# Convolution behind a group normalization: the first load of image 0 in two transfers

## The chip, the cores and the metric

The kernel runs on one core of a Trainium2 chip. A core has a matrix engine (TensorE, in the profile PE), a vector engine (VectorE, DVE), an activation engine (ScalarE, ACT), a general engine (GpSimd, POOL) and a sync engine (SP) that here issues all transfers. Data move between the chip's main memory and the on-chip memory (128 partitions) through sixteen DMA engines. The metric is the time of one execution in device microseconds, the median of several. For the kernel before it is 83.69 us (three executions, 83.59 to 84.02 us).

## The reference

The input `x` holds 8 images of 32 channels and 128 x 128 pixels in float32. Cut to what matters:

```python
def _gn(v, G=16, eps=1e-5):                 # mean and variance over 2 channels x 128 x 128 pixels
    g = v.reshape(B_, G, C_ // G, H_, W_)
    m = jnp.mean(g, axis=(2, 3, 4), keepdims=True)
    s = jnp.var(g, axis=(2, 3, 4), keepdims=True)
    return ((g - m) / jnp.sqrt(s + eps)).reshape(v.shape)

# a 3x3 convolution by FFT of size 256, cut to 128 x 128 at an offset of 64
sp = jnp.fft.ifft2(fout, norm='ortho').real
sh = (fft_H - out_h) // 2
sw = (fft_W - out_w) // 2
out = sp[:, :, sh:sh + out_h, sw:sw + out_w]
out = out + bias[None, :, None, None]

x = x + conv(_gn(x), L0_conv_weight, L0_conv_bias)
```

The offset of the cut makes the convolution reach only a quarter of the output; the rest of an image gets the bias alone. Every pixel is read once and written once: 16.8 MB in, 16.8 MB out.

## The kernel before

On the host, `x` is brought into the shape (4 pairs, 128 partitions, 2 images, 64 rows, 64 columns). A partition holds one channel at one parity of row and column. So one image is 128 partitions x 4096 numbers, and half an image 128 partitions x 2048 numbers (8192 bytes a partition).

All loads are issued by the sync engine one after the other, each with a semaphore of its own. Images 0 and 1 come in halves of 32 rows, the weights behind the first half:

```python
def load(to, of):
    name = f"load{len(put.sems)}"
    put.semaphore(name)
    return put("sp", lambda sp: sp.dma_start(to, of), adds=name)

for img in range(2):
    loaded[img] = []
    for half in range(2):
        rows = slice(half * H // 2, (half + 1) * H // 2)
        loaded[img].append((rows.stop, load(xts[img][:, rows, :], x[0, :, img, rows, :])))
        if img == 0 and half == 0:
            weights_in = load(wb_sb, wb)
for img in range(2):
    loaded[2 + img] = [(H, load(xts[2 + img], x[1, :, img]))]
for pair in range(2, NPAIR):
    loaded[2 * pair] = loaded[2 * pair + 1] = [(H, load(pairs[pair], x[pair]))]

def rows_in(img, last):          # the loads that hold rows before `last`
    return [token for k, (_, token) in enumerate(loaded[img]) if k == 0 or loaded[img][k - 1][0] < last]
```

The first instructions that need data wait for what `rows_in` names. For image 0 these are a small product on TensorE that estimates the mean (`pilot`), the sum of each half on VectorE and, with the origin from the pilot, the sum of squares of each half on ScalarE:

```python
def pilot(img):
    pilot_ok[img] = put(
        "pe", lambda e: e.matmul(ps_w[:, img : img + 1], avg, xts[img][:, 0, 0:1], start=True, stop=True),
        *rows_in(img, 1), avg_ok, mark=True,
    )
...
# sum_up(img), for each half k of image 0
e.tensor_reduce(to_sum(img, k)[:, 0:1], piece, mybir.AxisListType.X, ALU.add)      # waits rows_in(img, rows.stop)
# sum_squares(img)
e.activation(unused[...], piece, AF.Square, bias=origins[img], accum_out=to_sum(img, k)[:, 1:2])
```

From the sums follow mean and deviation (`group`, `take_std`), the normalized quarter `g` of the image (`normalize`), then twelve products per image on TensorE into PSUM (`multiply`, three chunks of four taps) and the addition to `x` (`add`). GpSimd adds the bias to the rest. The main loop works on one image while it prepares the next. Finished images go out through the same sync engine:

```python
def store(to, of, *needs):
    return put("sp", lambda sp: sp.dma_start(to, of), *needs, adds="stored")
...
xt, to = xts[B - 1], out[NPAIR - 1, :, 1]
store(to[:, N:H, :], xt[:, N:H, :], biased[B - 1][0])
add(B - 1, 0, 2)
add(B - 1, 2, NCHUNK)
stored = store(to[:, 0:N, :], xt[:, 0:N, :], biased[B - 1][1], *added[B - 1])
```

The kernel ends when all stores have landed.

Of the kernel before, what the change touches and what calls it, by code (L numbers as in the profile page):

```python
# [33 lines left out]
P = 128  # L34
# [113 lines left out]
def conv_preact_kernel(nc: bass.Bass, x: bass.AP, wb: bass.AP, out: bass.AP):  # L148
    NPAIR, _, _, H, W = x.shape
# [7 lines left out]
    def sbuf(name, *shape):  # L157
        return nc.alloc_sbuf_tensor(name, list(shape), F32).ap()
# [6 lines left out]
    pairs = [sbuf(f"x{pair}", P, 2, H, W) for pair in range(NPAIR)]  # L165
    xts = [pairs[img // 2][:, img % 2] for img in range(B)]
# [3 lines left out]
    loaded = {}  # L170
# [7 lines that stand above are left out]
        loaded[img] = []  # L178
        for half in range(2):
            rows = slice(half * H // 2, (half + 1) * H // 2)  # L180
            loaded[img].append((rows.stop, load(xts[img][:, rows, :], x[0, :, img, rows, :])))
            if img == 0 and half == 0:
                weights_in = load(wb_sb, wb)
    for img in range(2):
        loaded[2 + img] = [(H, load(xts[2 + img], x[1, :, img]))]
    for pair in range(2, NPAIR):
        loaded[2 * pair] = loaded[2 * pair + 1] = [(H, load(pairs[pair], x[pair]))]

    def rows_in(img, last):

        return [token for k, (_, token) in enumerate(loaded[img]) if k == 0 or loaded[img][k - 1][0] < last]

# [1 line left out]
    pair = sbuf("pair", P, P // 2, 2)  # L196
    w_sb = sbuf("w_sb", P, 4 * P)
    eps = sbuf("eps", P, 1)
    half = sbuf("half", P, 2 * C)
# [47 lines left out]
    def take_first(img, *needs):  # L247

        first_ok[img] = put(
            "pool", lambda e: e.tensor_copy(sums[(img - 1) % 2][:, 2:3], xts[img][:, 0, 0:1]),  # L250
            *rows_in(img, 1), *needs, *([group_ok[img - 3]] if img > 3 else []), mark=True,
# [8 lines that stand above are left out]
# [15 lines left out]
    def sum_up(img):  # L275
        sums_ok.setdefault(img, [])
        for k, rows in enumerate(parts(img)):
            piece = xts[img][:, rows, :].rearrange("p h w -> p (h w)")
            sums_ok[img].append(
                put(  # L280
                    "dve",
                    lambda e: e.tensor_reduce(to_sum(img, k)[:, 0:1], piece, mybir.AxisListType.X, ALU.add),  # L282
                    *rows_in(img, rows.stop), *([group_ok[img - 2]] if img > 1 else []), mark=True,
                )
            )
# [276 lines left out]
```

## Time and profile before

The page describes one execution, its span is 82.2 us.

| | kernel before |
|---|---|
| median time | 83.69 us |
| span of the profiled execution | 82.2 us |
| TensorE, VectorE, ScalarE, GpSimd busy | 81%, 61%, 58%, 37% of the span |
| DMA engines busy | 97.0% of the time of all sixteen |
| moved | 33.62 MB, mean 409 GB/s |
| first load (1024 KB): issued, landed | 0.81 us, 5.79 us |
| last store (1056 KB): issued, from issue to landing | 75.66 us, 6.5 us |

In the chain of waits each line has a start, a length and what ran, in microseconds from the start of the span. In the answers by window each line has the window, its length, the busy time (and number of instructions) of PE, PE's weight loads, DVE, ACT and POOL, then the granted clock of TensorE as a share, the busy share of the DMA engines and the GB/s that they moved. In short windows the share can exceed 1, since packets of one engine overlap a little. In the row of tenths one digit stands for a fortieth of the span.

### The profile page before, as it was taken

What the parts mean: (1) busy time and instruction counts of PE and PEld (TensorE: products, weight loads), DVE (VectorE), ACT (ScalarE), POOL (GpSimd) and SP (SyncE); (2) the same over time, 40 slices, a digit from 0 to 9 for tenths busy, and PEclk for the clock granted to TensorE, in tenths of its full rate; (3) what the DMA queues carried; (4) which work ended last, traced back from release to release, by engine and by line L of the source; (5) the groups of instructions that cost most, each with busy time, mean ns of one, the idle gap of its engine ahead of it and who ended that gap; (6) DMA issues with size and microseconds to landing.
All of it is one profiled execution on the core that took longest, in us unless ns stands there. A gap on an engine that the chain in (4) does not pass through costs nothing.

```text
span 82.2 us, 684 instructions
## 1 busy us (share of the span) xinstructions
PE 66.5 (81%) x222; PEld 41.3 (50%) x222; DVE 50.2 (61%) x43; ACT 48.0 (58%) x55; POOL 30.3 (37%) x41
## 2 busy tenths in 40 slices
PE   0019974999999999999999999999999999990000
PEld 0014443566666666666666666666666666650000
DVE  0019845971999499689949967994998341007000
ACT  6108957982797499479939956993896530000000
POOL 6808500000069910108984910770193059000000
PEclk9999998589999999999999999999999999999965
DMA  2899999999979979989959889999979999999994
GB/s 40 319 406 414 422 426 442 454 414 422 526 335 510 478 319 478 494 367 414 510 255 510 383 383 510 414 399 462 494 311 414 454 414 430 454 406 434 398 433 201
DMA packets 2208, 33.62 MB, mean 409 GB/s; under 512 B 256, under 2 KB 288, under 8 KB 416
## 3 DMA queue, kind: packets, MB, share of 16 engines
q1 hardware_dynamic: 2208, 33.62, 97.0%
HBM read 16.84 MB, written 16.78 MB: 409 GB/s over the span
## 4 chain that ended last, share of the span: by engine, by line
PE 75%; ACT 7%; DMA 6%; DVE 3%; issue 1%
PE ps L399 73%; DMA x<-x_dram 6%; ACT unused L302 5%; DVE x L415 2%; PE ps_m L317 2%; ACT g L360 1%; PE ps_w L257 1%; ACT std L340 0%; ACT square L329 0%; DVE rstd L346 0%; DVE var L334 0%; ACT origin L291 0%; DVE rstd L343 0%
## 5 line engine op out<-in xcount | busy, mean ns | idle before, releaser
L399 PE MATMUL ps<-g,w_sb 128*128 128x363 f32 (+1 forms) x192 | 60.7, 473 | 1.1 <-ACT g L360 1.1
L399 PEld LDWEIGHTS ps<-g,w_sb 128*128 128x128 f32 x192 | 36.0, 193 | 21.1 <-ACT origin L291 1.6
L282 DVE TENSOR_REDUCE sums<-x 128x1 f32<-128x4096 f32 x7 | 30.9, 4411 | 0.8 <-DMA x<-x_dram 0.8
L302 ACT ACTIVATE unused<-x,origin 128x4096 f32<-128x4096 f32 (+1 forms) x9 | 30.0, 3330 | 0.3
L381 POOL TENSOR_SCALAR x<-x,bias_sb 128x1984 f32<-128x1984 f32 (+3 forms) x12 | 23.2, 1949 | 18.1 <-ACT origin L291 13.8
L415 DVE SCALAR_TENSOR_TENSOR x<-ps,bias_sb,x 128x1089 f32<-128x1089 f32 (+2 forms) x9 | 10.9, 1221 | 7.6 <-PE ps L399 7.6
L360 ACT ACTIVATE g<-x,rstd 128x1089 f32<-128x1089 f32 (+2 forms) x9 | 10.7, 1201 | 3.9 <-DVE rstd L346 3.9
L282 DVE TENSOR_REDUCE first_sums<-x 128x1 f32<-128x2048 f32 x2 | 4.6, 2286 | 6.2 <-DMA x<-x_dram 6.2
L250 POOL COPY sums<-x 128x1 f32<-128x1 f32 x6 | 1.0, 185 | 18.0 <-DMA x<-x_dram 18.0
L334 DVE TENSOR_SCALAR var<-ps_m,square 128x1 f32<-128x1 f32 x8 | 1.7, 218 | 7.6 <-ACT square L329 7.6
L329 ACT ACTIVATE square<-ps_m,origin 128x1 f32<-128x1 f32 x8 | 2.1, 261 | 7.0 <-PE ps_m L317 7.0
L257 PE MATMUL ps_w<-x,avg 128*128 128x1 f32 x4 | 0.8, 278 | 5.9 <-DMA x<-x_dram 5.9
L433 PE MATMUL ps<-x,avg 128*128 128x512 f32 x6 | 4.9, 942 | 0.0
L257 PEld LDWEIGHTS ps_w<-x,avg 128*128 128x128 f32 x4 | 0.9, 250 | 6.4 <-issue 6.4
L317 PEld LDWEIGHTS ps_m<-sums,avg 128*128 128x128 f32 x16 | 2.8, 189 | 2.2 <-DVE x L415 1.0
L340 ACT ACTIVATE std<-var,eps 128x1 f32<-128x1 f32 x8 | 2.4, 294 | 2.3 <-DVE var L334 2.3
L343 DVE RECIPROCAL rstd<-std 128x1 f32<-128x1 f32 x8 | 1.3, 164 | 2.9 <-ACT std L340 2.9
L291 ACT ACTIVATE origin<-ps_w 128x1 f32<-128x1 f32 x2 | 0.3, 158 | 4.2 <-PE ps_w L257 4.2
L462 POOL COPY w_sb<-wb_sb 32x128 f32<-32x128 f32 (+1 forms) x8 | 2.5, 341 | 0.0
L317 PE MATMUL ps_m<-sums,avg 128*128 128x3 f32 x16 | 2.3, 214 | 0.0
L433 PEld LDWEIGHTS ps<-x,avg 128*128 128x128 f32 x6 | 1.5, 287 | 1.0 <-issue 1.0
L346 DVE TENSOR_SCALAR rstd<-ps_m,rstd 128x1 f32<-128x1 f32 x8 | 1.8, 219 | 0.3
(19 smaller groups left out, 10.4 us busy)
## 6 DMA issues: line engine op xcount, KB each, us to landing
x<-x_dram SPq DMA_DIRECT2D x2, 4096.0 KB, 33.6
out_dram<-x SPq DMA_DIRECT2D x2, 4096.0 KB, 16.4
out_dram<-x SPq DMA_DIRECT2D x3, 2048.0 KB, 9.1
x<-x_dram SPq DMA_DIRECT2D x4, 1024.0 KB, 7.8
x<-x_dram SPq DMA_DIRECT2D x2, 2048.0 KB, 17.4
out_dram<-x SPq DMA_DIRECT2D x1, 1056.0 KB, 6.5
out_dram<-x SPq DMA_DIRECT2D x1, 992.0 KB, 11.0
wb_sb<-wb_dram SPq DMA_DIRECT2D x1, 62.0 KB, 5.0
```

The lines of the kernel that those rows point to most:

```text
L257: "pe", lambda e: e.matmul(ps_w[:, img : img + 1], avg, xts[img][:, 0, 0:1], start=True, stop=True),
L282: lambda e: e.tensor_reduce(to_sum(img, k)[:, 0:1], piece, mybir.AxisListType.X, ALU.add),
L302: lambda e: e.activation(unused[:, rows.start * W : rows.stop * W], piece, AF.Square, bias=origins[img], accum_out=to_sum(img, k)[:, 1:2],),
L317: lambda e: e.matmul(ps_ms[:, 0 : of.shape[1]], avg, of, start=(part == 0), stop=(part == last)),
L329: lambda e: e.activation(squares[img], ps_ms[:, 0:1], AF.Square, bias=origins[img]),
L340: lambda e: e.activation(stds[img], variances[img], AF.Sqrt, bias=eps, scale=float(FFT * FFT)),
L360: lambda e: e.activation(g[:, rows, :], xt[:, LO + rows.start : LO + rows.stop, LO:W], AF.Identity, bias=rstd[:, 1:2], scale=rstd[:, 0:1],),
L381: put("pool", lambda e: e.tensor_scalar(part, part, 1.0, bias_sb, op0=ALU.mult, op1=ALU.add), *free, mark=mark)
L399: lambda e, k=k, dc=dc, rows=rows, top=top: e.matmul(ps[:, 0:rows, 0 : N - dc], w_sb[:, k * P : (k + 1) * P], g[:, top : top + rows, dc:N] ...
L415: lambda e: e.scalar_tensor_tensor(part, in0=ps, scalar=bias_sb, in1=part, op0=ALU.add, op1=ALU.add),
L433: "pe", lambda e: e.matmul(pss[1][:, 0, :], avg, piece, start=True, stop=True),
L462: lambda e: e.tensor_copy(w5[to, :, dc, :, c.start * C : c.stop * C], taps[:, 1 - rin : 5 - rin, b, :].rearrange("p (dr r) b o -> p dr r ( ...
```

## The change

The first half of image 0 is no longer one transfer of 128 partitions. It becomes a transfer of partitions 0 to 15, which gives each of the sixteen DMA engines a single row of 8192 bytes, and behind it a transfer of the other 112 partitions. The aim is that the engines get their first packets sooner. All other loads stay as they are. `loaded` now remembers the first row of each piece instead of the row behind its last, so that `rows_in` can name both pieces of the first half; for the other loads it names the same ones as before.

```diff
         for half in range(2):
             rows = slice(half * H // 2, (half + 1) * H // 2)
-            loaded[img].append((rows.stop, load(xts[img][:, rows, :], x[0, :, img, rows, :])))
+
+            for part in (slice(0, 16), slice(16, P)) if img == half == 0 else (slice(0, P),):
+                token = load(xts[img][part, rows, :], x[0, part, img, rows, :])
+                loaded[img].append((rows.start, token))
             if img == 0 and half == 0:
                 weights_in = load(wb_sb, wb)
     for img in range(2):
-        loaded[2 + img] = [(H, load(xts[2 + img], x[1, :, img]))]
+        loaded[2 + img] = [(0, load(xts[2 + img], x[1, :, img]))]
     for pair in range(2, NPAIR):
-        loaded[2 * pair] = loaded[2 * pair + 1] = [(H, load(pairs[pair], x[pair]))]
+        loaded[2 * pair] = loaded[2 * pair + 1] = [(0, load(pairs[pair], x[pair]))]
 
     def rows_in(img, last):
 
-        return [token for k, (_, token) in enumerate(loaded[img]) if k == 0 or loaded[img][k - 1][0] < last]
+        return [token for first, token in loaded[img] if first < last]
```

## The prediction

> **What bounds the kernel now.** I read three things in this order: what the DMA engines do over the whole span, the chain of waits together with its end, and the first microseconds in windows. First, from the page:
>
> ```profile
> span 82.2 us, 684 instructions
> PE 66.5 (81%) x222; PEld 41.3 (50%) x222; DVE 50.2 (61%) x43; ACT 48.0 (58%) x55; POOL 30.3 (37%) x41
> ...
> DMA  2899999999979979989959889999979999999994
> ...
> q1 hardware_dynamic: 2208, 33.62, 97.0%
> ```
>
> The packets of the only DMA queue fill 97.0% of the time of sixteen engines; TensorE is busy for 81%. The row of tenths has a low first slice, a slightly low second one, and then nothing that looks like a long pause until the last slice. The chain of work that ended last tells another story at first sight:
>
> ```profile
> 0.81 4.99 DMA x<-x_dram
> ...
> 13.43 6.17 PE ps L399 x14
> ...
> 71.11 3.01 PE ps L399 x10
> ...
> 74.15 1.48 DVE x L415 x2
> ```
>
> It says: wait for the first half of image 0 until 5.79 us, then statistics, then TensorE without a pause, then the last addition until 75.63 us. The span ends at 82.2 us, 6.5 us later, and the chain names no compute for that rest. The last store and the windows around it show why:
>
> ```profile
> 75.66 0.33 SPq L423 DMA_DIRECT2D out_dram<-x  x1
> ```
>
> ```profile
> 43.00:74.10 31.10, 31.10 (x111) 19.43 (x109) 20.05 (x18) 18.60 (x21) 12.46 (x10) 1.00 0.99 427
> 74.10:76.00 1.90, 0.01 (x1) 0.00 (x0) 1.48 (x2) 0.00 (x0) 0.00 (x0) 1.00 1.03 440
> 76.00:79.00 3.00, 0.00 (x0) 0.00 (x0) 0.00 (x0) 0.00 (x0) 0.00 (x0) 0.92 0.97 409
> 79.00:81.20 2.20, 0.00 (x0) 0.00 (x0) 0.00 (x0) 0.00 (x0) 0.00 (x0) 0.50 0.96 407
> ```
>
> The last column is GB/s, the one before it the busy share of the DMA engines. The last store (1056 KB) is issued at 75.66 us, but from 76 to 79 us the engines are still full with earlier stores. 1056 KB at the 427 GB/s of the steady stretch take about 2.5 us, so its data start near 81.2 - 2.5 = 78.7 us, although by the first load's example (issue 0.81, first packet about 1.82 us) it could have started near 76.7 us. So there are about 2 us of slack between the compute chain and the end. **The bound is the DMA stream**: it starts at 1.82 us, moves 33.62 MB, and never runs dry. What moves the end is the point at which each engine reaches its full rate, not the time at which the first tile lands. A shift of the first landing by less than 2 us changes the end only so far as it shifts the stream too.
>
> Now the start, in windows:
>
> ```profile
> 0.00:1.80 1.80, 0.00 (x0) 0.00 (x0) 0.00 (x0) 1.00 (x1) 1.13 (x7) 1.00 0.00 0
> 1.80:2.20 0.40, 0.00 (x0) 0.00 (x0) 0.00 (x0) 0.39 (x2) 0.33 (x2) 1.00 1.51 266
> 2.20:2.60 0.40, 0.00 (x0) 0.00 (x0) 0.00 (x0) 0.10 (x1) 0.40 (x1) 1.00 0.62 123
> 2.60:3.00 0.40, 0.00 (x0) 0.00 (x0) 0.00 (x0) 0.00 (x0) 0.32 (x2) 1.00 0.71 287
> 3.00:3.40 0.40, 0.00 (x0) 0.00 (x0) 0.00 (x0) 0.00 (x0) 0.32 (x2) 1.00 0.99 410
> 3.40:5.20 1.80, 0.00 (x0) 0.00 (x0) 0.00 (x0) 0.00 (x0) 0.60 (x2) 1.00 1.00 416
> ```
>
> Nothing moves before 1.8 us, the stream has its steady 410 GB/s only from 3.0 us. A packet is counted where it starts (nine packets of 8192 bytes start before 2.0 us, which is the 369 GB/s that the window 1.8 to 2.0 shows). In the trace's packet records the sixteen engines start their first packets between 1.82 and 2.35 us, on average 0.20 us after the first; these first packets take 0.37 to 1.17 us, 0.76 us on average, where a packet of the same size later takes 0.309 us. So the ramp costs an engine 0.20 us of stagger and 0.76 - 0.31 = 0.45 us of a slow first packet, about **0.65 us** in all. That is the whole pot of this change: 0.8% of the run. A gain over 2% (1.7 us) isn't there to be had.
>
> [...]
>
> **The change part by part.**
> Bytes: none added; 33.62 MB as before. Packets: the same 128 rows of 8192 bytes, and one more completion per engine at 9 ns: 0.01 us.
> Issue: one more DMA on the queue of the sync engine. The first was issued at 0.81 us, the second at 1.25 us, so one issue costs 0.44 us there. The 112 rows are issued at about 1.25 us, the weights and the rest 0.44 us later than before (last issue about 5.2 + 0.4 us instead of 5.2). The engines then hold work for tens of microseconds (the last load lands at 43 us), so only the 112 rows feel it: with the 1.01 us from issue to first packet they can start at about 2.26 us, and the last engine about 0.5 us later, 2.75 us.
> First packet: [...] I expect the stagger to shrink from 0.20 us to about 0.05 us on average: -0.15 us.
> Sharing: [...] For the engine that is last, nearly nothing, 0.0 to 0.1 us.
> The other 112: [...] One such meeting costs up to one packet, 0.31 us; I count half to one and a half of them for the engine that is last: 0.15 to 0.45 us. From the weights on the order is the old one, and each engine carries its delay to the end.
> Sum for the last engine, if the ports rule: +0.05 + 0.3 + 0.01, about **+0.4 us**.
> Waits: TensorE's first pilot product and VectorE's first sum wait for two semaphores instead of one; the list of instructions is otherwise the same on each engine, apart from the new wait. A few tens of ns, on the side with 2 us of slack: 0. First landing 5.79 us becomes about 6.1 us, and the TensorE chain shifts from 13.43 to about 13.8 us, also inside the slack.
>
> **The rivals.**
> *Rival 1, [...].* If the first packets are slow [...], then one row each starts all engines early, and the 112 rows arrive behind them in time. For it: the stagger of 0.5 us, and the very first packet, which took only 0.37 us. Against it: the durations don't grow in the order of the starts (the second packet to start took 0.91 us, the thirteenth 0.74 us). Then the stagger falls (-0.15 us) and up to half of the slow first packet (-0.2 us): 0.2 to 0.4 us below 83.69 us, 83.3 to 83.5 us.
> *Rival 2, hidden anyway.* The slow first reads belong to the first touch of the memory by each engine and stay, and the 112 rows come at 2.26 to 2.75 us, no sooner than the engines would have been free. The stagger moves from the first packet to the second: within 0.1 us of 83.69 us.
> *Rival 3, the queue's hole.* If the second transfer is served later than 2.75 us (a ramp of its own), each engine idles after its one packet; 0.2 to 0.6 us worse, and with the shared ports up to 84.5 us.
>
> **Range and chances.** Shared ports with +0.4 us or more get a little over half of my belief, the hidden case a fifth, the gain of 0.2 to 0.4 us a quarter. Weighted: 0.55 x 0.4 + 0.2 x 0 - 0.25 x 0.3, about +0.15 us; I take +0.2 us, since the engine that is last decides: **83.9 us**. The range from 83.3 us (rival 1 nearly whole) to 84.5 us (ports and hole together) should hold it 8 times in 10. 2% is 1.7 us, 2.6 times the pot: faster 0.01, same 0.97, slower 0.02.
>
> **What would show it.** In the windows from 1.8 to 3.4 us: with shared ports sixteen packets start within some 0.15 us of each other, [...]. With rival 1 they take 0.3 to 0.5 us and 410 GB/s are reached before 2.8 us. With rival 3 the DMA share drops to zero between the two transfers. The first sum on VectorE starts at about 6.1 us (shared ports), 5.5 us (rival 1) or 5.8 us (rival 2). The last store must still find the engines busy with earlier stores, and the end must move as the stream does. I am wrong in the bound, not only in the ramp, if the first sum and the end move in opposite ways, or if the end moves by more than the 0.65 us of the pot in the gainful direction.

## The result, and the profile after

The changed kernel takes 84.59 us (median of six, 84.49 to 84.68), the kernel before 83.72 us beside it. The ratio is 1.0097 with a 95% interval of 1.007 to 1.0123, so the change costs 0.9 us by the medians, 0.6 to 1.0 us by the interval. The predicted 83.9 us had the sign right, but was far too small, and the range (83.3 to 84.5 us) ends below the result.

First the page of the changed kernel, the same lines as shown of the kernel before:

```profile
span 83.2 us, 686 instructions
...
DMA  1899999999996997999699799979969999999993
...
q1 hardware_dynamic: 2224, 33.62, 96.6%
```

Sixteen more packets (2208 to 2224) are the completions of the extra transfer; the bytes are the same, the DMA engines are still the fullest thing on the core, and the first slice is a little emptier. The chain of waits of the changed kernel, in order of time:

```profile
1.25 5.77 DMA x<-x_dram
...
14.61 6.17 PE ps L402 x14
...
72.30 3.01 PE ps L402 x10
...
75.34 1.48 DVE x L418 x2
```

The first half of image 0 is complete at 7.02 us instead of 5.79 (+1.23), TensorE starts its products at 14.61 us instead of 13.43 (+1.18), and every later piece has the same length as before. The end moved by only 83.2 - 82.2 = 1.0 us. That the chain still isn't what sets the end shows in the last store, which is issued late in a queue that is still full:

```profile
76.85 0.33 SPq L426 DMA_DIRECT2D out_dram<-x  x1
```

```profile
76.00:79.00 3.00, 0.00 (x0) 0.00 (x0) 0.82 (x2) 0.00 (x0) 0.00 (x0) 1.00 0.93 395
79.00:81.20 2.20, 0.00 (x0) 0.00 (x0) 0.00 (x0) 0.00 (x0) 0.00 (x0) 0.70 1.01 426
```

The store before it lands between 79.6 and 80.6 us. With 1.01 us from issue to the first packet, as for the first load of the kernel before (0.81 to 1.82 us), the last store could have begun near 77.9 us; it had to wait for the stream.

So the question is where the stream was delayed. The windows of the start, changed kernel:

```profile
1.80:2.20 0.40, 0.00 (x0) 0.00 (x0) 0.00 (x0) 0.39 (x2) 0.33 (x2) 1.00 1.07 287
2.20:2.60 0.40, 0.00 (x0) 0.00 (x0) 0.00 (x0) 0.10 (x1) 0.40 (x1) 1.00 1.82 287
2.60:3.00 0.40, 0.00 (x0) 0.00 (x0) 0.00 (x0) 0.00 (x0) 0.32 (x1) 1.00 0.28 41
3.00:3.40 0.40, 0.00 (x0) 0.00 (x0) 0.00 (x0) 0.00 (x0) 0.32 (x1) 1.00 0.61 205
3.40:5.20 1.80, 0.00 (x0) 0.00 (x0) 0.00 (x0) 0.00 (x0) 0.59 (x2) 1.00 1.00 323
5.20:6.00 0.80, 0.00 (x0) 0.00 (x0) 0.00 (x0) 0.00 (x0) 0.00 (x0) 1.00 0.95 262
```

Three things are to be seen. More packets start before 2.6 us than before (287 GB/s in the second window instead of 123), which is what the change was made for. Then there is a hole: nearly nothing starts from 2.6 to 3.0 us. (A packet's whole time and bytes count in the window in which it starts, hence a share of 1.82 in one window and 0.28 in the next; most engines are still busy with what they began before.) And, the long part: from 3.4 to 6.0 us the engines are fully busy (share 1.00 and 0.95) while only 323 and 262 GB/s start, where the kernel before had 416 and 384. Its line for the second of these windows:

```profile
5.20:6.00 0.80, 0.07 (x1) 0.10 (x1) 0.18 (x1) 0.00 (x0) 0.00 (x0) 1.00 1.04 384
```

So from 3.4 to 5.2 us a busy share of 1.00 stands beside 416 GB/s in the kernel before and beside 323 GB/s here.

The packet records of the trace give the sizes. The sixteen packets of the small transfer took 0.31 to 0.58 us, 0.47 us on average, less than a first packet before (0.76). But their completions (small packets of 4 bytes, which ended by the record between 2.39 and 2.58 us) arrive between 3.34 and 3.75 us, 1.06 us later on average; for image 3's load that takes 0.47 us. Of the next sixteen, the first of the 112 rows, fourteen started between 2.39 and 2.67 us and took 0.72 to 1.27 us; the other two engines started theirs only at about 3.23 us. The remaining rows took 0.37 us on average at first and 0.46 us towards the end; in the kernel before a packet of this size takes 0.31 us (309 ns) from 3.0 us on.

### The profile page after: what moved, and what is told of

Its sections match the earlier page's. It is cut to its first block, busy times and chain, and to the rows that moved or that the text cites. A ratio compares the mean times of both kernels' runs of the same rounds, so it can differ in the third digit from the quotient of the medians.

```text
span 83.2 us, 686 instructions
## 1 busy us (share of the span) xinstructions
PE 66.6 (80%) x222; PEld 41.3 (50%) x222; DVE 50.2 (60%) x43; ACT 48.0 (58%) x55; POOL 30.2 (36%) x41
## 2 busy tenths in 40 slices
DMA packets 2224, 33.62 MB, mean 404 GB/s; under 512 B 272, under 2 KB 304, under 8 KB 432
## 3 DMA queue, kind: packets, MB, share of 16 engines
q1 hardware_dynamic: 2224, 33.62, 96.6%
## 4 chain that ended last, share of the span: by engine, by line
PE 74%; DMA 7%; ACT 7%; DVE 3%; issue 1%; SPq 0%
PE ps L402 72%; DMA x<-x_dram 7%; ACT unused L305 5%; DVE x L418 2%; PE ps_m L320 2%; ACT g L363 1%; PE ps_w L260 1%; SPq L175 0%; ACT std L343 0%; ACT square L332 0%; DVE var L337 0%; DVE rstd L349 0%; ACT origin L294 0%; DVE rstd L346 0%
## 5 line engine op out<-in xcount | busy, mean ns | idle before, releaser
L461 POOL COPY bias_sb<-wb_sb 32x1 f32<-32x1 f32 x4 | 0.7, 180 | 3.4 <-DMA wb_sb<-wb_dram 3.3
```

## The experiments

Three theories stood for the loss. *Ports* (in the prediction: shared ports): how long a packet takes depends on the partitions that its transfer writes, and pieces of 16 and 112 partitions are slower than one of all 128. The name stands for a supposition of the author's; what the runs can show is the partitions and the times. *Start*: the second transfer is issued 0.44 us later and has a ramp of its own. *Odd count*: 112 rows are slower because 112 is not a power of two.

All times of the experiments are compared by ratio with the kernel before on the same chip. Since the end hides small things, I also use a measure in the trace: the mean landing of image 3's load (its sixteen completions), at 22.99 us in the kernel before. It lies behind everything that the change touches and before the first store. In the changed kernel it is 24.11 us, **1.12 us later**. It comes from one execution of each kernel. How far such a number scatters can be seen at image 1's first half: in five kernels that issue the same loads up to there its mean landing lies between 10.67 and 10.74 us.

### The cut moved to a later load

```diff
-            for part in (slice(0, 16), slice(16, P)) if img == half == 0 else (slice(0, P),):
+            for part in (slice(0, 16), slice(16, P)) if img == half == 1 else (slice(0, P),):
```

(The condition `img == half == 1` picks the second half of image 1, not of image 0 as the expectation says; that load, too, comes at full rate, after 10 us; from 6 to 9 us the windows of this run show 415 GB/s.)

> The first half of image 0 in one transfer again; its second half, which comes when the engines have been at full rate for 2 us, is cut into partitions 0 to 15 and 16 to 127. Theory ports [...]: the cost comes along, +0.6 to +1.1 us over the kernel before, and the packets of the 112 rows take 0.37 to 0.5 us each. Theory start (the second transfer is issued 0.44 us later and has a ramp of its own): nothing left to lose, the time of before within 0.2 us, packets of 0.31 us. Theory odd count (112 is not a power of two and is laid out slowly): like ports in time, but with gaps between packets instead of long ones.

Measured: 86.11 us, ratio 1.0221 (1.0129 to 1.0313), about +1.9 us; image 3's load lands 2.55 us later. Packets of 0.31 us give way to longer ones between 10 and 15.5 us (0.44 to 0.80 us on average, taken by the microsecond). *Start* falls: there is no ramp here, and the loss is larger, not smaller. The size is twice what I expected of *ports*, as if the ramp had hidden part of the cost in the changed kernel.

### Two transfers of 64

```diff
-(slice(0, 16), slice(16, P))
+(slice(0, 64), slice(64, P))
```

> The first half of image 0 in two transfers of 64 partitions each. Theory ports: [...] the first half lands near 7 to 7.8 us instead of 5.8 and the end comes +1.2 to +2.2 us later than before. Theory start: [...] within 0.2 us of before. Theory odd count: 64 is a power of two, within 0.2 us of before.

Measured: 85.94 us, ratio 1.0201 (1.0117 to 1.0285), about +1.7 us; image 3's load +2.39 us. After the start all packets of this half take 0.56 to 0.61 us on average, twice the usual. The windows of this kernel:

```profile
3.40:5.20 1.80, 0.00 (x0) 0.00 (x0) 0.00 (x0) 0.00 (x0) 0.59 (x2) 1.00 1.05 237
5.20:6.00 0.80, 0.00 (x0) 0.00 (x0) 0.00 (x0) 0.00 (x0) 0.00 (x0) 1.00 1.22 266
```

A full share of busy engines with 237 GB/s, where the kernel before had 416. *Odd count* would have had no cost with 64, *start* neither.

### A cut by image rows instead of partitions

```diff
-            for part in (slice(0, 16), slice(16, P)) if img == half == 0 else (slice(0, P),):
-                token = load(xts[img][part, rows, :], x[0, part, img, rows, :])
-                loaded[img].append((rows.start, token))
+            pieces = [slice(rows.start, 4), slice(4, rows.stop)] if img == half == 0 else [rows]
+            for piece in pieces:
+                token = load(xts[img][:, piece, :], x[0, :, img, piece, :])
+                loaded[img].append((piece.start, token))
```

> The first half of image 0 in two transfers of all 128 partitions each: image rows 0 to 3 (1024 bytes a partition), then rows 4 to 31. Theory ports: [...] no loss; within 0.2 us of before, or up to 0.3 us faster if small first packets shorten the ramp. Theory start: the second transfer is issued 0.44 us later here as well, with only 128 KB ahead of it, so +0.5 to +0.9 us as in the changed kernel. Theory odd count: no loss.

Measured: 83.92 us, ratio 0.9997 (0.9978 to 1.0015): no difference at the end; image 3's load lands 0.25 us later. Two transfers, 128 KB in the first and the second issued 0.44 us later, just as in the change, but each with all 128 partitions. So neither the second transfer nor its later issue costs what the change lost: 0.25 of its 1.12 us at image 3's load, and nothing at the end. Nothing was gained either. The start of this kernel:

```profile
2.20:2.60 0.40, 0.00 (x0) 0.00 (x0) 0.00 (x0) 0.10 (x1) 0.40 (x1) 1.00 1.74 364
2.60:3.00 0.40, 0.00 (x0) 0.00 (x0) 0.00 (x0) 0.00 (x0) 0.32 (x2) 1.00 0.77 143
3.00:3.40 0.40, 0.00 (x0) 0.00 (x0) 0.00 (x0) 0.00 (x0) 0.32 (x2) 1.00 0.65 251
3.40:5.20 1.80, 0.59 (x2) 0.50 (x2) 0.00 (x0) 0.17 (x1) 0.60 (x2) 1.00 1.00 403
```

Packets for 364 GB/s start from 2.2 to 2.6 us (123 in the kernel before), but the first packets of the large transfer behind the 128 small ones were slow again (0.67 us on average, up to 1.25 us), so the full rate comes at 3.4 us instead of 3.0.

### 112 partitions first, then 16

```diff
-(slice(0, 16), slice(16, P))
+(slice(0, P - 16), slice(P - 16, P))
```

> The two pieces of the first half in the other order and place: partitions 0 to 111 first, then 112 to 127. Theory ports: the 112 rows cost as much as in the changed kernel, [...]: +0.9 to +1.6 us over before. Theory start: the first transfer is as large as before and covers the later issue of the second, so within 0.2 us of before. Theory odd count: about as the changed kernel, +0.6 to +1 us.

Measured: 85.00 us, ratio 1.0134 (1.0111 to 1.0158), about +1.1 us; image 3's load +1.43 us. As *ports* has it, and worse than the changed kernel: there the 16 rows lie in the ramp, here behind it. *Start* expected nothing.

### The same bytes into partitions 0 to 15, every eighth and all 128

These three and the next leave the kernel before as it is and add loads that nothing reads, into a spare tile. They come behind image 1, at full rate (397 to 426 GB/s from 11 to 13 us in these four runs); the last store waits for them. A theory *source*, by which the rows read decide and not the partitions written, expects the same cost of the first two. First four loads of 16 rows into neighbouring partitions:

```diff
+    for k in range(4):
+        extras.append(load(spare[0:16, k * 2048 : (k + 1) * 2048], x[0, 0:16, 0, 0:32, :].rearrange(...)))
```

> The kernel before with extra work: ahead of images 2 and 3 four more loads of 16 rows of 8192 bytes (512 KB in all) into partitions 0 to 15 of a spare tile that nothing reads. Theory ports: [...] the end comes +4 to +5 us later. Theory source (the sixteen engines are slowed by where they read, not by where they write): [...]. Theory odd count: 16 is a power of two, +1.2 to +1.5 us.

Then the same source rows into every eighth partition:

```diff
-spare[0:16, k * 2048 : (k + 1) * 2048]
+spare[0:128:8, k * 2048 : (k + 1) * 2048]
```

> The same four extra loads of the same 16 rows, into every eighth partition (0, 8, ... 120), [...]. Theory ports: [...] +2.0 to +2.7 us. [...] Theory odd count: +1.2 to +1.5 us.

And as control the same number of bytes in one load of all partitions:

```diff
+    extras.append(load(spare[:, 0:1024], x[0, :, 0, 0:16, :].rearrange(...)))
```

> The control: the same 512 KB extra in one load of 128 partitions of 4096 bytes. Every theory: the price of the bytes alone, 512 KB at 427 GB/s, +1.2 us (1.1 to 1.5).

| extra 512 KB | ratio (95%) | time, us | image 3's load later by |
|---|---|---|---|
| partitions 0 to 15 | 1.0629 (1.0578 to 1.0681) | 88.86 | 5.02 us |
| every eighth | 1.0364 (1.0324 to 1.0404) | 86.64 | 2.74 us |
| all 128 | 1.0151 (1.0105 to 1.0197) | 84.94 | 1.29 us |

Two of these ends come later than *ports* had it: about +5.3 us (4 to 5 expected) and +3.0 us (2.0 to 2.7 expected). The windows while these loads run; first partitions 0 to 15:

```profile
13.00:14.00 1.00, 0.64 (x2) 0.53 (x3) 0.00 (x0) 1.00 (x2) 0.00 (x0) 0.90 1.09 115
14.00:15.00 1.00, 1.00 (x3) 0.48 (x3) 0.64 (x1) 0.86 (x3) 0.00 (x0) 0.50 0.86 90
```

then every eighth partition:

```profile
13.00:14.00 1.00, 0.63 (x1) 0.39 (x2) 0.28 (x1) 1.00 (x2) 0.00 (x0) 0.76 1.10 229
14.00:15.00 1.00, 1.00 (x3) 0.68 (x2) 1.00 (x1) 0.90 (x3) 0.00 (x0) 0.50 1.39 295
```

and the control:

```profile
13.00:14.00 1.00, 1.00 (x4) 0.40 (x3) 0.33 (x2) 0.80 (x2) 0.00 (x0) 1.00 1.26 512
14.00:15.00 1.00, 1.00 (x2) 0.73 (x3) 1.00 (x1) 0.90 (x3) 0.00 (x0) 1.00 0.90 381
```

The packet records say it more sharply. In the kernel before, whose loads of 8192 bytes a row write all 128 partitions, a packet takes 0.31 us from 3.0 us on. From 13 to 16 us the packets to partitions 0 to 15 take 1.19 to 1.22 us on average, four times as long; from 13 to 15 us those to every eighth partition take 0.60 to 0.63 us, twice as long.

All sixteen engines are busy with the four loads in both of the first two kernels (busy shares 1.09 and 0.86, 1.10 and 1.39 from 13 to 15 us). The source rows, the number of engines, the sizes and the count of transfers are the same; only the partitions written differ, and the cost nearly halves. That settles for 16 rows that the place written decides. The 512 KB put image 3's load off by 5.02 us at partitions 0 to 15, which is 104 GB/s. *Odd count* falls for 16, and *source* for both.

### The 112 rows by themselves

```diff
+    extras.append(load(spare[16:P, 0:2048], x[0, 16:P, 0, 0:32, :].rearrange(...)))
```

> The kernel before with one extra load at the same place: 112 rows of 8192 bytes (896 KB) into partitions 16 to 127 of the spare tile, the second piece of the change by itself and at full rate. The bytes alone are 2.15 us. Theory ports: [...] each engine's packets take 0.4 to 0.5 us, so +2.8 to +3.8 us, 0.7 to 1.6 us above the price of the bytes. Theory start: +2.1 to +2.4 us, the 112 rows are no slower than others once the engines run.

Measured: 87.13 us, ratio 1.0417 (1.0385 to 1.0449), about +3.5 us; image 3's load +3.45 us. By the control, 896 KB cost 1.29 x 896 / 512 = 2.26 us, so 1.19 us are the shape. The windows of this kernel:

```profile
13.00:14.00 1.00, 1.00 (x4) 0.68 (x3) 0.27 (x1) 1.00 (x2) 0.00 (x0) 1.00 1.03 287
14.00:15.00 1.00, 1.00 (x2) 0.50 (x2) 1.00 (x1) 0.90 (x3) 0.00 (x0) 1.00 1.05 287
```

The engines are busy without gaps at 287 GB/s; each engine's first packet of this load took 0.35 us on average, the later six 0.44 to 0.52 us. *Odd count* expected gaps between packets and falls. No run gives the 112 rows from the same source another place, as was done for the 16; that it is the place here too is carried over from them.

### Each piece in the ramp

The same two loads into the spare tile, now issued ahead of everything; first the 16 rows, then, in a kernel of its own, the 112:

```diff
+    extras.append(load(spare[0:16, 0:2048], x[0, 0:16, 0, 0:32, :].rearrange(...)))
     for img in range(2):
         loaded[img] = []
```

> The kernel before with one extra load of 16 rows of 8192 bytes into partitions 0 to 15 of a spare tile, issued ahead of everything, so the first piece of the change by itself, in the ramp, with the whole of the first half behind it in one transfer of 128. At full rate such a load cost 5.24 / 4 = 1.31 us. Theory ports, with the ramp hiding part of it: 1.31 us less the 0.65 us that the ramp loses anyway, +0.5 to +0.9 us. Rival, nothing hidden: +1.2 to +1.5 us. Rival, the small first piece costs nothing in the ramp: at most the price of its bytes, +0.3 us, and then all the loss of the change is in the 112 rows.

> The kernel before with one extra load of 112 rows of 8192 bytes into partitions 16 to 127 of the spare tile, issued ahead of everything, so the second piece of the change by itself, in the ramp. At full rate it cost 3.5 us. Theory ports, with its slow first packets lying in the ramp: +2.8 to +3.3 us. Rival, the ramp hides nothing: +3.4 to +3.6 us. Rival, [...]: near the price of the bytes, +2.2 to +2.5 us.

Measured: 16 rows ahead 84.32 us, ratio 1.0058 (1.0029 to 1.0088), about +0.5 us; image 3's load +0.56 us. 112 rows ahead 86.54 us, ratio 1.0309 (1.0219 to 1.0399), about +2.6 us; image 3's load +3.04 us; at the end that is a little less than *ports* had it (2.8 to 3.3). Less the price of the bytes by the control (0.32 and 2.26 us):

| cost of the shape, us, at image 3's load | at full rate | in the ramp |
|---|---|---|
| 16 rows, partitions 0 to 15 | 5.02 / 4 - 0.32 = 0.93 | 0.56 - 0.32 = 0.24 |
| 112 rows | 3.45 - 2.26 = 1.19 | 3.04 - 2.26 = 0.78 |
| sum | 2.12 | **1.02** |
| both together, measured | 2.55 (cut in image 1) | **1.12** (the changed kernel) |

In the ramp the parts account for 1.02 of the 1.12 us of the changed kernel, and the 112 rows are three quarters of that. Two cautions. The sum counts what the ramp hides once for each piece, and at full rate the parts leave 0.4 us of the pair unexplained, so the close agreement may be luck in part. And the 0.24 us of the 16 rows are no more than the 0.25 us that the cut by image rows showed with a small first transfer of all 128 partitions: in the ramp nothing of the narrow shape is to be seen, the cost is the same as that of a small transfer ahead that writes all 128 partitions. The packet records of the changed kernel itself agree. On the average engine the third packet starts about 0.3 us later than before (3.42 against 3.12 us), and the eighth ends about 0.9 us later (5.93 against 5.01 us), so about 0.6 us arise within the later six of the seven rows.

### The ramp

Why are first packets slow at all? The first load was held back, with everything else unchanged:

```diff
-loaded[img].append((rows.stop, load(xts[img][:, rows, :], x[0, :, img, rows, :])))
+loaded[img].append((rows.stop, load(xts[img][:, rows, :], x[0, :, img, rows, :], avg_ok)))
```

> The kernel before with its first load held back until GpSimd has the averaging matrix, so that it is issued at about 3.5 us instead of 0.8. If the slow first packets (0.76 us on average) belong to the first big transfer, they are as slow again, only later, and the end comes about 2.7 us later. If they belong to what else goes on in the first 3 us of the execution, they take 0.31 to 0.4 us now and the end comes only 2.2 to 2.4 us later.

Measured in one execution: the load is issued at 3.55 us (+2.74), the first sixteen packets take 0.61 us on average. So the slow start goes for the most part with the first large transfer, and not with the first 3 us of the execution; image 3's load lands 2.60 us later, so 0.14 us of the 0.65 us of the ramp may have gone. One engine fell 1.2 to 2 us behind the others in this run (the mean of the last landings is 2.9 us later than before, the latest 4.4 us), which made its 87.92 us; why, isn't known.

From the hidden cost of the 16 rows I then tried a version that might beat both kernels, the weights ahead of the first half instead of behind it:

```diff
+    weights_in = load(wb_sb, wb)
     for img in range(2):
         loaded[img] = []
...
-            if img == 0 and half == 0:
-                weights_in = load(wb_sb, wb)
```

> The kernel before with the weights [...] issued ahead of the first half instead of behind it. Theory ports, with the ramp hiding part of what a narrow transfer costs, as it hid 0.7 us of the 16 rows: [...], 0.1 to 0.3 us faster than before. Rival, the ramp is bound to the first big transfer: it simply starts 0.44 us later behind a small one, as in the run with image rows 0 to 3 ahead, and the time is that of before or up to 0.3 us more.

Measured: 84.22 us, ratio 1.0047 (1.0021 to 1.0072), 0.4 us slower (0.2 to 0.6); image 3's load +0.23 us. The first packets of the large transfer begin at 2.36 us or later and again take 0.79 us on average. The rival was nearer: with the small piece ahead the ramp moved and wasn't filled. No version here beats the kernel before.

## Why the prediction was wrong

**The bound: right.** The DMA stream sets the end. The compute chain moved by 1.2 us, the last store still waited behind the earlier ones, and loads that nothing reads (the control, for one: ratio 1.0151, image 3's load 1.29 us later) lengthen the run by about their price.

**The issue: right but for a small hole.** 0.44 us per transfer, first sum of two waits: the cut by image rows has both, and at its end nothing of them is to be seen. Rival 3's hole between the transfers exists on two of the sixteen engines, which begin on the 112 rows only at about 3.23 us; the other fourteen begin between 2.39 and 2.67 us. The empty windows from 2.6 to 3.0 us come one packet later, while engines are busy with long packets.

**The stagger: half right.** I wrote 0.20 to 0.05 us. The sixteen starts now spread from 1.83 to 2.26 us, on average 0.15 us after the first: a gain of 0.05 us, not 0.15.

**Sharing (the 16 rows): a cost at full rate, hidden in the ramp.** At full rate the packets of 16 rows into partitions 0 to 15 take 1.19 to 1.22 us. In the ramp they took 0.47 us, and only the completions are late (1.06 us instead of 0.47); why, isn't shown. The next packet, 0.85 us on average, is no sign of a cost of these partitions, since the first large packets behind a small transfer of 128 partitions are about as slow (0.67 us, the cut by image rows). I put the effect on the engine that is last at 0 to 0.1 us beyond the stagger, an estimate that no trace stood behind. Alone in the ramp the 16 rows cost 0.24 us, but the small first transfer of all 128 partitions costs as much there (0.25 us); this cost of a small transfer ahead was missing from the sum.

**The other 112: the term that failed.** The prediction said "One such meeting costs up to one packet, 0.31 us; I count half to one and a half of them for the engine that is last: 0.15 to 0.45 us." The runs showed 0.78 us in the ramp and 1.19 us at full rate in its place, so this term was mis-sized by a factor of about two to five. It isn't a delay of one packet here and there: all rows got longer, from 0.31 us to 0.37 at first and 0.46 at the end. That such delays come singly, and how many of them fall on one engine, was the author's estimate and in no trace. Nor do these runs show how the rows are dealt to the engines, only that the shape costs this much; why it costs that much stays open.

**The weights of the rivals: wrong too.** A quarter of the belief was in a gain of 0.2 to 0.4 us from a shorter ramp. It took 0.25 x (0.4 + 0.3), about 0.18 us, off the +0.4 us of the shared ports, and the fifth in the hidden case another 0.08 us: that is how +0.4 became +0.15, rounded to +0.2. The cut by rows and the weights ahead show that no such gain was there: behind the small packets the first large ones are slow all the same (0.67 and 0.79 us on average). Rival 2 ("hidden anyway") was nearest in this respect. But without these weights the prediction would still have been +0.4 us.

**What I didn't have: a part given back.** The stream was 1.12 us late at image 3's load, but only 0.82 us late at the last load (43.54 us against 42.72), and the mean of the last landings is 0.66 us later (82.32 against 81.66). In the kernel before, each engine has one packet of 32 KB, started between 40.6 and 41.0 us, that took 1.29 to 1.99 us instead of 1.21. The changed kernel has none above 1.27 us, the cut by rows and the control have it again. It lies where loads are about to give way to stores; its cause was not tried. In the changed kernel, on the other hand, one engine falls behind among the stores, and the latest landing is 0.97 us later. So the 0.9 us at the end is 1.12 us of loss less what these two make of it.

## What to carry to other kernels

Judge a transfer by the partitions it writes, not by the number of engines it keeps busy: here, with all sixteen engines busy, the same 512 KB cost 5.02 us into partitions 0 to 15 and 2.74 us into every eighth, and one load of 512 KB into all 128 cost 1.29 us. If a load must be cut, cut it along its free dimension and keep the 128 partitions whole; here that cost nothing at the end (83.92 us, ratio 0.9997), and gained nothing. Where a queue never runs dry, read GB/s beside the busy share (1.00 with 416 GB/s in the kernel before, 1.00 with 323 in the changed one), and look at the end for the stream's delay rather than at the first wait.

## What the runs showed of the hardware

- The time of a packet went with the partitions that its load wrote: packets of 8192 bytes took 0.31 us in loads of all 128 partitions, 0.60 to 0.63 us in loads of 16 rows into every eighth, and 1.19 to 1.22 us in loads of 16 rows into partitions 0 to 15.
- The completions of a transfer came well after its packets ended by the record: for sixteen packets of 0.47 us into partitions 0 to 15 they came 1.06 us after the end of their own records, for image 3's load 0.47 us. Why the first are so late isn't shown.
- The slow first packets (0.76 us on average instead of 0.31) belong for the most part to the first large transfer: they followed it when it was held back by 2.74 us (0.61 us, one execution) and when small packets went ahead (up to 1.25 us in one case, 0.79 us on average in the other). What they wait for stays open.
- The cost of a narrow load disappeared in that slow start: 16 rows into partitions 0 to 15 cost 0.93 us beyond the price of their bytes at full rate, and as the first transfer 0.24 us, no more than a small first transfer of all 128 partitions (0.25 us).
